# A conv-seq block on one core: LayerNorm transposes by VectorE in 32x32 blocks and through DRAM instead of by TensorE

## The chip, the cores and the metric

The kernel runs on one core of one Trainium2 chip. The metric is device time in microseconds (us), the median of several executions. The core has five engines that run beside each other and meet at semaphores: TensorE (PE in the profile; its weight loads are shown apart as PEld), VectorE (DVE), ScalarE (ACT), GpSimd (POOL) and SyncE (SP), which here only issues DMAs.

## What is computed

The input is `x` of 2 x 256 x 128 x 128 in float32: batch, time T, band FB, channel C. Three sublayers follow each other, each with a LayerNorm in front and a residual sum behind it:

```python
xt = _ln(x, ln_t_w, ln_t_b).transpose(0, 2, 1, 3)
x = x + _mha(xt, t_wi, t_bi, t_wo, t_bo, H_T, cm).transpose(0, 2, 1, 3)   # over time, causal, 4 heads of 32
xf = _ln(x, ln_f_w, ln_f_b)
x = x + _mha(xf, f_wi, f_bi, f_wo, f_bo, H_F, bm)                          # over bands, |i - j| <= 16, 4 heads
xn = _ln(x, ln_n_w, ln_n_b)
h = jax.nn.gelu(xn @ w1.T + b1, approximate=False)                         # 128 -> 512
x = x + (h @ w2.T + b2)                                                    # 512 -> 128
```

## The kernel before

**Groups.** The work is cut into groups of 512 tokens (NT = 4 tiles of 128 tokens by 128 channels). There are 384 of them. First come 128 groups of the attention over time (`OverTime`; two bands with all their 256 times each). They write an intermediate `x1` to DRAM. Then come 128 groups of the attention over bands (`OverBands`; four times with all 128 bands) and 128 of the feed-forward layer (`FeedForward`), in turns of 8 and 8: 16 runs of 8 band groups and then the same 8 groups' feed-forward. This document calls these the time stage, the band iterations and the feed iterations.

**Steps of a group.** `load` brings x (one tile for several groups). `statistics` takes mean and variance on DVE (`stats`, `mv`), `root` takes the power -1/2 on POOL (`rstd`), and `normalize` writes `xh` on DVE, with tokens on the partitions. Matrix products need channels on the partitions. So `transpose` turns the four 128x128 tiles of `xh` on PE into a PSUM bank `xp`, and `take_transposed` copies it to SBUF on ACT as `xnT`. From `xnT` come the products `qp`, `kp`, `vp` in an attention group (copied out as `qT`, `kT`, `v`) and `hp` in a feed group. An attention group goes on with the scores `sp` (PE), their exponentials `pt` or `pf` (ACT), masks (POOL `affine_select`; for bands the last head by a DVE product with `band`), row sums `rp` and weighted values `op` (PE; `weigh`), the inverse of the sums by `ln` and `r` (ACT; `invert`), `t`, `u`, `oT` (DVE; `divide`), the output product `yp` (PE; `output`) and the residual sum (DVE; `finish`). In the time stage POOL also adds two blocks of `pt` for the first half of the scores, and DVE for the second (`last_sum`). POOL forms the residual plus bias (`bias`; `rd` in the time stage). A feed group has `hp`, the Gelu `hT` (ACT), `zp` (PE) and the residual sum `res` (DVE).

**Order.** `BoundedPath.run` writes the order out by hand, as a software pipeline: iteration n works on the scores of group n, on the sums of group n-1, on the output of n-2, on `qp`/`kp`/`vp` of n+1, on the LayerNorm of n+2 and n+3, and loads for n+10. PE, DVE, ACT and POOL keep exactly this program order (`InOrder`), so an instruction that waits holds up everything behind it on its engine. Only the DMAs on SP are placed by the scheduler, and SP too runs its list in order. All PSUM tiles share eight banks that are handed out in turn. So a product that opens a bank waits for the reader of the tile eight openings earlier.

**Numerics.** All is float32. An ordinary product shows as two MATMULs in the trace, a transpose as one.

Another path for large weights (`shifted_path`) is in the program and isn't taken with these inputs.

Of the kernel before, what the change touches and what calls it, by code (L numbers as in the profile page):

```python
# [2 lines left out]

# [6 lines left out]
F32 = mybir.dt.float32  # L10
# [8 lines left out]
P = 128  # L19
H = 4  # L20
# [402 lines left out]


class Group:


# [78 lines left out]
    def take_key(self):  # L506
        pass
# [23 lines left out]
class Attention(Group):  # L531
    which = None

    def bias(self):
        self.dst_tile()
# [4 lines left out]
    def dst_tile(self):  # L540
        pass

# [57 lines left out]
    def finish(self):  # L600
        self.path.vector.tensor_tensor(self.dst(), self.yp, self.dst(), ALU.add)
        if self.store is not None:
            self.store(self.dst())


def rows_of(h):
    return slice(h * D, (h + 1) * D)


class OverTime(Attention):  # L610
# [5 lines left out]
    W = 3 * P  # L616

    def dst_tile(self):
        rd = self.path.work.tile([P, NT, P], F32, name="rd", bufs=5)
        self.dst = lambda: rd  # L620

# [80 lines left out]
class OverBands(Attention):  # L702
# [33 lines left out]

    def take_key(self):
        path = self.path
        self.kT = path.work.tile([P, NT * P], F32, name="kT")
        path.scalar.copy(self.kT, self.kp)  # L740

    def first_half(self):
# [19 lines left out]
class FeedForward(Group):  # L762

    def bias(self):
        path = self.path
        self.res = path.work.tile([P, NT, P], F32, name="res")
        path.gpsimd.tensor_tensor(
            self.res, self.src(), path.k.rows[:, 2:3, :].to_broadcast([P, NT, P]), ALU.add
        )
# [36 lines left out]
    def divide(self):  # L806
        self.path.vector.tensor_tensor(self.res, self.zp, self.res, ALU.add)
        self.store(self.res)

# [16 lines left out]
class BoundedPath:  # L826
    def __init__(self, ctx, tc, k):
# [18 lines left out]
    def bank(self, shape, name):  # L846
        return self.ps.tile(shape, F32, name=name, tag="ps")

    def groups(self, x, out):
        nc, k = self.nc, self.k  # L850
        B, T, FB, C = x.shape
        NC_T = T // P
        S = NT // NC_T
        for b in range(B):
            xv = x[b].rearrange("(o p) f c -> p o f c", p=P)
            x1v = k.x1[b].rearrange("(o p) f c -> p o f c", p=P)
            for f0 in range(0, FB, GA):
                held = {}

                def load(f0=f0, xv=xv, held=held):  # L860
                    held["x"] = self.xpool.tile([P, GA, NC_T, C], F32, name="xt", tag="x")
                    for o in range(NC_T):
                        nc.sync.dma_start(held["x"][:, :, o, :], xv[:, o, f0 : f0 + GA, :])

                for g in range(0, GA, S):

                    def src(g=g, held=held):
                        return held["x"][:, g : g + S].rearrange("p f o c -> p (f o) c")

                    def store(t, f=f0 + g, x1v=x1v):  # L870
                        for o in range(NC_T):
                            nc.sync.dma_start(
                                x1v[:, o, f : f + S, :],
                                t.rearrange("p (f o) c -> p f o c", o=NC_T)[:, :, o, :],
                            )

                    yield OverTime(self, src, None, load if g == 0 else None, store)
        for b in range(B):
            x1v = k.x1[b].rearrange("t f c -> f t c")
            outv = out[b].rearrange("t f c -> f t c")  # L880
            for r0 in range(0, T, RUN):
                run = []
                for t0 in range(r0, r0 + RUN, GB):
                    held = {}

                    def load(t0=t0, x1v=x1v, held=held):
                        held["x"] = self.xpool.tile([P, GB, C], F32, name="xb", tag="x")
                        nc.sync.dma_start(held["x"], x1v[:, t0 : t0 + GB, :])
                        held["x2"] = self.xpool.tile([P, GB, C], F32, name="x2", tag="x2", bufs=2 * RUN // GB)

                    def part(name, g, held=held):
                        return lambda: held[name][:, g : g + NT, :]

                    def store(t, g, outv=outv):
                        nc.sync.dma_start(outv[:, g : g + NT, :], t)

                    run += [(t0 + g, part("x", g), part("x2", g), None if g else load, store) for g in range(0, GB, NT)]
                for i, (_, x_, x2, load, _) in enumerate(run):
                    g = OverBands(self, x_, x2, load)
                    if i == len(run) - 1:  # L900
                        g.by_vector = 2
                    yield g
                for g, _, x2, _, store in run:
                    yield FeedForward(self, x2, None, None, lambda t, g=g, store=store: store(t, g))

    def run(self, x, out):
# [9 lines left out]

        self.scalar.preload_act_table_set(EXP_SET)
        for n in range(-10, len(groups) + 2):
            feeds = [at(n - 2 + i, FeedForward) for i in range(5)]
            bands = [at(n - 2 + i, OverBands) for i in range(5)]  # L920
            do(n + 10, "load")
            do(n + 3, "statistics")
            if bands[2] and feeds[1]:
                self.scalar.preload_act_table_set(EXP_SET)
            do(n, "first_half", "first_function", "first_mask")
            do(n + 2, "normalize")
            do(n + 3, "root")
            if bands[2]:
                do(n, "second_mask")
            if feeds[2] and feeds[3]:  # L930
                do(n + 1, "transpose", "take_transposed")
            do(n - 1, "weigh")
# [4 lines left out]
            do(n - 1, "divide")  # L937
            if feeds[3] and not feeds[2]:
                do(n + 1, "transpose", "take_transposed")
            do(n, "second_half", "second_function")  # L940
            if not bands[2]:
                do(n, "second_mask", "bias")
                if at(n + RUN // NT, OverBands):
                    do(n + RUN // NT, "bias")
                do(n - 2, "output", "finish")
            do(n + 1, "queries_keys", "take_query", "take_key", "values", "take_values")
            do(n, "last_sum")
            if at(n + 2, Attention):
                do(n + 2, "transpose", "take_transposed")

# [68 lines left out]
```

## Time and profile before

| | |
|---|---|
| median of 3 executions | 2968.1 us (2967.6 to 2968.57) |
| the profiled execution | 2968.23 us, of which its span is 2966.3 us |
| busy share of the span | PE 99%, DVE 65%, ACT 68%, POOL 69% |
| granted clock of TensorE | 0.999 of full speed |
| DMA | 140.41 MB, 16.0% of the 16 DMA engines' time on the SP queue |

Rows give the line as L821 for everything that `InOrder` records, so tile names, not lines, tell operations apart (in the changed kernel the same line is L827). A row of the timeline has the start in us from the span's start, the duration, the engine, the operation with its tiles and shapes, the count of merged instructions and, in brackets, the idle time before it and what ended it. A row of the groups has the count, the busy time in all, the mean duration in ns, and the idle time before. PE rows overlap, because matmuls are pipelined: the time that a step costs on PE is the distance from its start to the next start.

### The profile page before, as it was taken

What the parts mean: (1) busy time and instruction counts of PE and PEld (TensorE: products, weight loads), DVE (VectorE), ACT (ScalarE), POOL (GpSimd) and SP (SyncE); (2) the same over time, 40 slices, a digit from 0 to 9 for tenths busy, and PEclk for the clock granted to TensorE, in tenths of its full rate; (3) what the DMA queues carried; (4) which work ended last, traced back from release to release, by engine and by line L of the source; (5) the groups of instructions that cost most, each with busy time, mean ns of one, the idle gap of its engine ahead of it and who ended that gap; (6) DMA issues with size and microseconds to landing.
All of it is one profiled execution on the core that took longest, in us unless ns stands there. A gap on an engine that the chain in (4) does not pass through costs nothing.

```text
span 2966.3 us, 75357 instructions
## 1 busy us (share of the span) xinstructions
PE 2929.6 (99%) x30246; PEld 2082.9 (70%) x30246; DVE 1933.7 (65%) x6206; ACT 2007.6 (68%) x3664; POOL 2057.4 (69%) x2537
## 2 busy tenths in 40 slices
PE   7999999999999999999999999999999999999998
PEld 5666666666666677777777777777777777767776
DVE  6777777777777895646647557466465475564663
ACT  4777777777777776756657657567576576675664
POOL 5888888888888896656657656566576575665662
PEclk9999999999999999999999999999999999999999
DMA  3222222222222221111111111111101011111001
GB/s 84 64 62 62 76 62 62 73 66 62 63 79 62 62 69 37 37 44 30 44 29 37 40 34 41 40 33 41 42 28 48 26 37 40 33 41 44 15 16 30
DMA packets 222855, 140.41 MB, mean 47 GB/s; under 512 B 7968, under 2 KB 205984, under 8 KB 222496
## 3 DMA queue, kind: packets, MB, share of 16 engines
q1 hardware_dynamic: 221248, 134.45, 16.0%
q8 instruction: 240, 3.93, 0.6%
q10 hardware_dynamic: 1248, 1.05, 0.1%
q14 instruction: 119, 0.97, 0.1%
HBM read 68.36 MB, written 67.11 MB: 46 GB/s over the span
## 4 chain that ended last, share of the span: by engine, by line
PE 99%; ACT 0%; DMA 0%; DVE 0%; POOL 0%; issue 0%; SPq 0%; ACTq 0%; POOLq 0%; DVEq 0%
PE zp L821 16%; PE hp L821 15%; PE sp L821 12%; PE op L821 9%; PE yp L821 9%; PE rp L821 9%; PE vp L821 8%; PE qp L821 8%; PE kp L821 7%; PE xp L821 6%; ACT xnT L821 0%; DMA xt<-in_x 0%; DMA f_wiT_sb<-in_f_wiT 0%; POOL pt L821 0%; POOL rstd L821 0%
## 5 line engine op out<-in xcount | busy, mean ns | idle before, releaser
L821 POOL TENSOR_SCALAR_AFFINE_SELECT pf<-pf 128x512 f32<-128x512 f32 x736 | 508.2, 705 | 277.1 <-ACT pf L821 252.0
L821 ACT ACTIVATE hT<-hp,b 128x512 f32<-128x512 f32 x512 | 346.6, 687 | 463.7 <-PE hp L821 460.2
L821 PE MATMUL hp<-xnT,w1f 128*128 128x512 f32 x1024 | 474.4, 596 | 10.8 <-ACT xnT L821 10.8
L821 POOL TENSOR_TENSOR rstd<-rstd,mhalf 128x4 f32<-128x4 f32 x384 | 460.6, 1200 | 32.0
L821 PE MATMUL zp<-w2T_sb,hT 128*128 128x128 f32 x4096 | 480.3, 276 | 0.1
L821 PEld LDWEIGHTS zp<-w2T_sb,hT 128*128 128x128 f32 x4096 | 469.0, 192 | 10.2 <-issue 8.1
L821 ACT ACTIVATE pt<-sp 128x384 f32<-128x384 f32 x1024 | 419.7, 497 | 75.2 <-PE sp L821 42.3
L821 POOL TENSOR_SCALAR_AFFINE_SELECT pt<-pt 128x512 f32<-128x512 f32 x512 | 312.7, 632 | 153.0 <-ACT pt L821 153.0
L821 PE MATMUL sp<-qT,kT 32*128 32x128 f32 (+1 forms) x8192 | 389.6, 316 | 0.0
L821 DVE TENSOR_TENSOR res<-zp,res 128x512 f32<-128x512 f32 x128 | 88.3, 690 | 452.9 <-issue 365.6
L821 POOL TENSOR_SCALAR rstd<-mv 128x4 f32<-128x4 f32 x384 | 94.2, 245 | 397.1 <-DVE mv L821 397.1
L821 PEld LDWEIGHTS sp<-qT,kT 32*128 32x128 f32 x8192 | 311.3, 185 | 72.5 <-issue 40.1
L821 PEld LDWEIGHTS vp<-wf,xnT 128*128 128x128 f32 x2048 | 269.2, 192 | 122.4 <-issue 113.8
L821 DVE TENSOR_TENSOR t<-rp,r 128x512 f32<-128x512 f32 x256 | 175.4, 685 | 215.0 <-ACT r L821 213.4
L821 ACT ACTIVATE pf<-sp 128x512 f32<-128x512 f32 x512 | 264.3, 603 | 57.2 <-POOL rstd L821 32.5
L821 PEld LDWEIGHTS hp<-xnT,w1f 128*128 128x128 f32 x1024 | 180.1, 191 | 171.0 <-issue 151.6
L821 PE MATMUL yp<-wn,oT 128*128 128x128 f32 x2048 | 293.4, 287 | 0.0
L821 PEld LDWEIGHTS yp<-wn,oT 128*128 128x128 f32 x2048 | 250.6, 191 | 49.8 <-issue 18.6
L821 DVE TENSOR_TENSOR pf<-pf,band 128x512 f32<-128x512 f32 x144 | 142.6, 999 | 214.4 <-ACT pf L821 214.4
L821 PE MATMUL vp<-wf,xnT 128*128 128x128 f32 x2048 | 270.0, 275 | 0.0
L821 ACT COPY v<-vp 128x512 f32<-128x512 f32 x256 | 149.8, 585 | 173.9 <-PE vp L821 173.9
L821 PE MATMUL qp<-xnT,wf 128*128 128x512 f32 x512 | 265.0, 600 | 0.7 <-ACT xnT L821 0.7
(94 smaller groups left out, 5053.1 us busy)
## 6 DMA issues: line engine op xcount, KB each, us to landing
xt<-in_x SPq DMA_DIRECT2D x64, 512.0 KB, 5.4
x<-rd SPq DMA_DIRECT2D x256, 128.0 KB, 1.9
out<-res SPq DMA_DIRECT2D x128, 256.0 KB, 2.3
xb<-x SPq DMA_DIRECT2D x32, 0.5 KB, 6.1
w1T_sb<-in_w1T ACTq DMA_DIRECT2D x1, 256.0 KB, 3.8
w2T_sb<-in_w2T ACTq DMA_DIRECT2D x1, 256.0 KB, 4.2
t_wiT_sb<-in_t_wiT ACTq DMA_DIRECT2D x1, 192.0 KB, 2.6
f_wiT_sb<-in_f_wiT ACTq DMA_DIRECT2D x1, 192.0 KB, 3.7
```

Of the source, the lines that this page charges most:

```text
L821: return self.tc.keep_in_program_order(emit(*args, **kwargs))
```

## The change

1. The PE transposes (`xp`) and the ACT copies `xnT<-xp` go, in all 384 groups. In their place `turn` transposes 32x32 blocks of `xh` within each of the four 32-partition rows on DVE, one instruction of 128x512 into a tile `z`. Four DMAs of 64 KB each, one for each 32-partition row, write `z` to a DRAM tile `turned`. `fetch` reads the 256 KB back as `xnT` with one DMA over 128 partitions. `turn` is done three iterations ahead and `fetch` two.
2. A 32x32 transpose can't move data between 32-partition rows. So tokens lie differently on the chip: a group's partition row i holds 32 tokens of each of four stretches, instead of a tile holding 128 neighbours. Loads and stores go in four DMAs over 32 partitions each, for four groups (loads) or two groups (stores) at a time. `xnT` has its columns in the old token order. `t`, `u` and the Gelu's `hT` are written in the new one (`by_rows`), so that the output products give rows in the new layout.
3. In the time stage `kT<-kp` moves from DVE to ACT (in the band iterations it is on ACT already). `output` and `finish` of group n-2 move behind `queries_keys` of n+1.
4. The residual tile is `res`, four groups wide, in both the time stage and the feed iterations. Loads are issued 11 iterations ahead and statistics taken 4 ahead.

```diff
-        self.xh = path.work.tile([P, NT, P], F32, name="xh", bufs=4)
+        self.xh = path.work.tile([P, NT, P], F32, name="xh", bufs=2)
...
-    def transpose(self):
-
-        path = self.path
-        self.xp = path.bank([P, NT * P], "xp")
+    def turn(self):
+
+
+        path = self.path
+        z = path.work.tile([P, H, P], F32, name="z", bufs=2)
+        path.vector.transpose(
+            z.rearrange("p c (t q) -> p c t q", q=D), self.xh.rearrange("p t (c q) -> p c t q", q=D)
+        )
+        self.turned = path.dram.tile([H, D, NT, P], F32, name="turned")
         for i in range(NT):
-            path.tensor.transpose(self.xp[:, i * P : (i + 1) * P], self.xh[:, i, :], path.k.ident)
-
-    def take_transposed(self):
+            path.nc.sync.dma_start(self.turned[:, :, i, :].rearrange("c a x -> a c x"), z[rows_of(i)])
+
+    def fetch(self):
         path = self.path
         self.xnT = path.work.tile([P, NT * P], F32, name="xnT")
-        path.scalar.copy(self.xnT, self.xp)
+        path.nc.sync.dma_start(self.xnT, self.turned.rearrange("c a i x -> (c a) (i x)"))
...
-        path.vector.tensor_copy(self.kT, self.kp)
+        path.scalar.copy(self.kT, self.kp)
...
-        vector.tensor_tensor(t, self.rp, self.r0, ALU.mult)
+        vector.tensor_tensor(by_rows(t), by_tile(self.rp), by_tile(self.r0), ALU.mult)
         u = path.work.tile([P, NT * P], F32, name="u", bufs=2)
-        vector.tensor_tensor(u, self.op, self.r0, ALU.mult)
+        vector.tensor_tensor(by_rows(u), by_tile(self.op), by_tile(self.r0), ALU.mult)
...
-            path.scalar.activation(self.hT[:, j, :], self.hp[j], AF.Gelu, bias=path.k.b1[:, j : j + 1], scale=1.0)
+            path.scalar.activation(
+                by_rows(self.hT[:, j, :]), by_tile(self.hp[j]), AF.Gelu,
+                bias=path.k.b1[:, j : j + 1], scale=1.0,
+            )
...
+        self.dram = ctx.enter_context(tc.tile_pool(name="turns", bufs=3, space=DRAM))
...
+                    for i in range(2 * g, min(2 * g + 2, NT)):
+                        f = f0 + i // NC_T * NT
+                        nc.sync.dma_start(held["x"][rows_of(i)], self.of_times(x[b], i, slice(f, f + NT)))
...
+                    for i in range(NT if g % 2 else 0):
+                        f = f0 + i // NC_T * NT + g
+                        nc.sync.dma_start(
+                            self.of_times(k.x1[b], i, slice(f - 1, f + 1)), held["res"][rows_of(i), :, g - 1 : g + 1]
+                        )
...
-            do(n + 10, "load")
-            do(n + 3, "statistics")
+            do(n + 11, "load")
+            do(n + 4, "statistics")
...
-            do(n + 2, "normalize")
-            do(n + 3, "root")
+            do(n + 2, "fetch")
+            do(n + 3, "normalize", "turn")
+            do(n + 4, "root")
...
-            if feeds[2] and feeds[3]:
-                do(n + 1, "transpose", "take_transposed")
...
-            if feeds[3] and not feeds[2]:
-                do(n + 1, "transpose", "take_transposed")
...
+            do(n + 1, "queries_keys", "take_query", "take_key")
+            if not bands[2]:
                 do(n - 2, "output", "finish")
-            do(n + 1, "queries_keys", "take_query", "take_key", "values", "take_values")
+            do(n + 1, "values", "take_values")
             do(n, "last_sum")
-            if at(n + 2, Attention):
-                do(n + 2, "transpose", "take_transposed")
```

The order on three engines shows what the scheduler made of it. PE, one iteration of the time stage (the second scores, the output of an earlier group, the products of the next group, its first scores), before:

```order
L821 MATMUL sp<-qT,kT 128x128 x4
L821 MATMUL yp<-wn_106,oT 128x128 x4
L821 MATMUL qp<-xnT,wf_103 128x512
L821 MATMUL kp<-xnT,wf_103 128x512
L821 MATMUL vp<-wf_103,xnT 128x128 x4
L821 MATMUL xp<-ident,xh 128x128 x4
L821 MATMUL sp<-qT,kT 128x256 x4
L821 MATMUL sp<-qT,kT 128x128 x4
L821 MATMUL rp<-pt,ones 32x512 x4
```

And of the change:

```order
L827 MATMUL sp<-qT,kT 128x128 x4
L827 MATMUL qp<-xnT,wf_103 128x512
L827 MATMUL kp<-xnT,wf_103 128x512
L827 MATMUL yp<-wn_106,oT 128x128 x4
L827 MATMUL vp<-wf_103,xnT 128x128 x4
L827 MATMUL sp<-qT,kT 128x256 x4
L827 MATMUL sp<-qT,kT 128x128 x4
L827 MATMUL rp<-pt,ones 32x512 x4
```

The four transposes are gone, and `yp` stands between `kp` and `vp`.

DVE in the same stage, from `divide` to the next `divide`, before:

```order
L821 SCALAR_TENSOR_TENSOR oT<-t,u 128x512
L821 TENSOR_TENSOR rd<-yp,rd 128x512
L821 COPY kT<-kp 128x512
L821 TENSOR_TENSOR pt<-pt 128x4x128
L821 BN_STATS stats<-xt 128x6 x4
L821 BN_AGGR mv<-stats 128x2 x4
L821 TENSOR_SCALAR xh<-xt,mv,rstd 128x128 x4
L821 TENSOR_TENSOR t<-rp,r_1795 128x512
```

And of the change (the residual tile is now `res`):

```order
L827 SCALAR_TENSOR_TENSOR oT<-t,u 128x512
L827 TENSOR_TENSOR res<-yp,res 128x4x128
L827 TENSOR_TENSOR pt<-pt 128x4x128
L827 BN_STATS stats<-x 128x6 x4
L827 BN_AGGR mv<-stats 128x2 x4
L827 TENSOR_SCALAR xh<-x,mv,rstd 128x128 x4
L827 STREAM_TRANSPOSE z<-xh 128x512
L827 TENSOR_TENSOR t<-rp,r_1738 128x4x4x32
```

The copy of `kT` has left DVE, and the block transpose stands between `xh` and `t`.

SP's list of DMAs for four groups of the time stage, of the change (before, the same stretch held two loads and eight stores):

```order
L489 DMA turned<-z 32x4x128 x4
L494 DMA xnT<-turned 128x512
L489 DMA turned<-z 32x4x128 x4
L494 DMA xnT<-turned 128x512
L890 DMA x_0_85<-res 32x4x256 x4
L489 DMA turned<-z 32x4x128 x4
L494 DMA xnT<-turned 128x512
L489 DMA turned<-z 32x4x128 x4
L494 DMA xnT<-turned 128x512
L890 DMA x_0_85<-res 32x4x256 x4
L885 DMA x<-in_x 32x4x512 x4
```

Each `fetch` stands right behind the four writes that it must wait for, so SP holds everything behind it until they have landed.

More of the change, by code (lines that the diff above doesn't have):

```diff
@@ L2 @@
 from contextlib import ExitStack
+from functools import partial
 import concourse.bass as bass
@@ L422, in fold, with by_rows, by_tile @@
     return nc.values_load(flag[0:1, 0:1], min_val=0, max_val=1)
+def by_rows(t):
+    return t.rearrange("p (t i q) -> p i t q", i=NT, q=D)
+def by_tile(t):
+    return t.rearrange("p (i t q) -> p i t q", i=NT, q=D)
 class Group:
@@ L534, in bias @@
     def bias(self):
-        self.dst_tile()
         self.path.gpsimd.tensor_tensor(
@@ L538, in bias @@
         )
-    def dst_tile(self):
-        pass
     def queries_keys(self):
@@ L602, in finish @@
         if self.store is not None:
-            self.store(self.dst())
+            self.store()
 def rows_of(h):
@@ L735, in second_mask @@
             path.vector.tensor_tensor(blk, blk, path.band.unsqueeze(1).to_broadcast([P, NT, P]), ALU.mult)
-    def take_key(self):
-        path = self.path
-        self.kT = path.work.tile([P, NT * P], F32, name="kT")
-        path.scalar.copy(self.kT, self.kp)
     def first_half(self):
@@ L765, in bias @@
         path = self.path
-        self.res = path.work.tile([P, NT, P], F32, name="res")
         path.gpsimd.tensor_tensor(
-            self.res, self.src(), path.k.rows[:, 2:3, :].to_broadcast([P, NT, P]), ALU.add
+            self.dst(), self.src(), path.k.rows[:, 2:3, :].to_broadcast([P, NT, P]), ALU.add
         )
@@ L806, in divide @@
     def divide(self):
-        self.path.vector.tensor_tensor(self.res, self.zp, self.res, ALU.add)
-        self.store(self.res)
+        self.path.vector.tensor_tensor(self.dst(), self.zp, self.dst(), ALU.add)
+        self.store()
 class InOrder:
@@ L847, in bank, with of_times, of_bands, quad @@
         return self.ps.tile(shape, F32, name=name, tag="ps")
+    @staticmethod
+    def of_times(ap, i, f):
+        o = ap.shape[0] // P
+        return ap.rearrange("(o t q) f c -> o q t f c", o=o, q=D)[i % o][:, :, f]
+    @staticmethod
+    def of_bands(ap, a, n):
+        return ap[a : a + n].rearrange("t (m q) c -> q (t m) c", q=D)
+    def quad(self, held, name, bufs):
+        held[name] = self.xpool.tile([P, NT, NT, P], F32, name=name, tag=name, bufs=bufs)
     def groups(self, x, out):
@@ L852, in groups, with load @@
         NC_T = T // P
-        S = NT // NC_T
         for b in range(B):
-            xv = x[b].rearrange("(o p) f c -> p o f c", p=P)
-            x1v = k.x1[b].rearrange("(o p) f c -> p o f c", p=P)
             for f0 in range(0, FB, GA):
                 held = {}
[L860 to L877, printed above, removed]
+                def load(g, f0=f0, b=b, held=held):
+                    if g == 0:
+                        self.quad(held, "x", 4)
+                    for i in range(2 * g, min(2 * g + 2, NT)):
+                        f = f0 + i // NC_T * NT
+                        nc.sync.dma_start(held["x"][rows_of(i)], self.of_times(x[b], i, slice(f, f + NT)))
@@ new lines, in store, with part @@
+                def store(g, f0=f0, b=b, held=held):
+                    for i in range(NT if g % 2 else 0):
[3 more added lines that the diff above has]
+                        )
+                def part(name, g, held=held):
+                    if name == "res" and name not in held:
+                        self.quad(held, "res", 2)
+                    return held[name][:, :, g]
@@ L878, in groups @@
+                for g in range(NT):
+                    yield OverTime(self, partial(part, "x", g), partial(part, "res", g), partial(load, g), partial(store, g))
         for b in range(B):
-            x1v = k.x1[b].rearrange("t f c -> f t c")
-            outv = out[b].rearrange("t f c -> f t c")
             for r0 in range(0, T, RUN):
@@ L884, in groups @@
                     held = {}
[L886 to L889, printed above, removed]
-                    def part(name, g, held=held):
-                        return lambda: held[name][:, g : g + NT, :]
-                    def store(t, g, outv=outv):
-                        nc.sync.dma_start(outv[:, g : g + NT, :], t)
@@ L897, in groups, with load @@
-                    run += [(t0 + g, part("x", g), part("x2", g), None if g else load, store) for g in range(0, GB, NT)]
-                for i, (_, x_, x2, load, _) in enumerate(run):
-                    g = OverBands(self, x_, x2, load)
+                    def load(g, t0=t0, b=b, held=held):
+                        if g == 0:
+                            self.quad(held, "x", 4)
+                            self.quad(held, "x2", 2 * RUN // GB)
+                        for i in range(2 * g, min(2 * g + 2, NT)):
+                            nc.sync.dma_start(
+                                held["x"][rows_of(i)].rearrange("q g t c -> q (g t) c"),
+                                self.of_bands(k.x1[b], t0 + NT * i, NT),
+                            )
@@ new lines, in store @@
+                    def store(g, t0=t0, b=b, held=held):
+                        for i in range(NT if g % 2 else 0):
+                            nc.sync.dma_start(
+                                self.of_bands(out[b], t0 + NT * i + g - 1, 2),
+                                held["res"][rows_of(i), g - 1 : g + 1].rearrange("q g t c -> q (g t) c"),
+                            )
+                    def part(name, g, held=held):
+                        if name == "res" and name not in held:
+                            self.quad(held, "res", 2)
+                        return held[name][:, g]
@@ L900, in groups @@
+                    run += [(g, part, load, store) for g in range(NT)]
+                for i, (g, part, load, _) in enumerate(run):
+                    group = OverBands(self, partial(part, "x", g), partial(part, "x2", g), partial(load, g))
                     if i == len(run) - 1:
[L901 to L904, printed above, removed]
+                        group.by_vector = 2
+                    yield group
@@ L906, in run @@
+                for g, part, _, store in run:
+                    yield FeedForward(self, partial(part, "x2", g), partial(part, "res", g), None, partial(store, g))
     def run(self, x, out):
@@ L917, in run @@
         self.scalar.preload_act_table_set(EXP_SET)
-        for n in range(-10, len(groups) + 2):
+        for n in range(-11, len(groups) + 2):
             feeds = [at(n - 2 + i, FeedForward) for i in range(5)]
             bands = [at(n - 2 + i, OverBands) for i in range(5)]
-            do(n + 10, "load")
-            do(n + 3, "statistics")
+            do(n + 11, "load")
+            do(n + 4, "statistics")
             if bands[2] and feeds[1]:
```

3 lines of the change are left out of this document (removed).

## The prediction

> **What bounds the kernel now.** I read the page first: busy shares, and the chain that ended last.
>
> ```profile
> PE 2929.6 (99%) x30246; PEld 2082.9 (70%) x30246; DVE 1933.7 (65%) x6206; ACT 2007.6 (68%) x3664; POOL 2057.4 (69%) x2537
> PE 99%; ACT 0%; DMA 0%; DVE 0%; POOL 0%; issue 0%; SPq 0%; ACTq 0%; POOLq 0%; DVEq 0%
> PE zp L821 16%; PE hp L821 15%; PE sp L821 12%; PE op L821 9%; PE yp L821 9%; PE rp L821 9%; PE vp L821 8%; PE qp L821 8%; PE kp L821 7%; PE xp L821 6%; ACT xnT L821 0%; DMA xt<-in_x 0%; DMA f_wiT_sb<-in_f_wiT 0%; POOL pt L821 0%; POOL rstd
> ```
>
> TensorE is the bound: its busy time is the span, and the chain runs from PE to PE. The transposes `xp` are 6% of that chain, some 178 us. The other engines' 65 to 69% are averages over three stages. So I went to the timeline of each stage for two things: what a transpose really costs on PE, and how much room the others keep once an iteration is shorter.
>
> **What PE loses.** One iteration of the time stage, PE alone:
>
> ```profile
> 399.89 0.94 PE L821 MATMUL sp<-qT,kT 32*128 32x256 f32 x16
> ...
> 403.05 0.94 PE L821 MATMUL sp<-qT,kT 32*128 32x256 f32 x16
> ...
> 406.63 1.05 PE L821 MATMUL vp<-wf,xnT 128*128 128x128 f32 x8
> 407.52 0.60 PE L821 MATMUL xp<-ident,xh 128*128 128x128 f32 x4
> 408.05 0.94 PE L821 MATMUL sp<-qT,kT 32*128 32x256 f32 x16
> 408.91 1.07 PE L821 MATMUL rp<-pt,ones 128*32 128x512 f32 x8
> ```
>
> From the first `sp` to that of the next iteration it is 8.16 us. `xp` takes 0.53 to the next start, but `vp` straight to `sp` isn't free: the last band iteration of each run happens to have no `xp` there.
>
> ```profile
> 2058.80 1.02 PE L821 MATMUL kp<-xnT,wf 128*128 128x512 f32 x2
> 2059.66 1.05 PE L821 MATMUL vp<-wf,xnT 128*128 128x128 f32 x8
> 2060.55 0.60 PE L821 MATMUL xp<-ident,xh 128*128 128x128 f32 x4
> 2061.08 1.17 PE L821 MATMUL sp<-qT,kT 32*128 32x128 f32 x32
> ...
> 2065.91 1.02 PE L821 MATMUL kp<-xnT,wf 128*128 128x512 f32 x2
> 2066.76 1.05 PE L821 MATMUL vp<-wf,xnT 128*128 128x128 f32 x8
> 2067.75 1.17 PE L821 MATMUL sp<-qT,kT 32*128 32x128 f32 x32
> ```
>
> From `kp` to `sp` it is 2.28 us with the transposes and 1.84 without: **0.44 us** a group. A feed iteration agrees (from `xp` to `zp` 0.43):
>
> ```profile
> 1994.76 0.60 PE L821 MATMUL xp<-ident,xh 128*128 128x128 f32 x4
> 1995.19 3.74 PE L821 MATMUL zp<-w2T_sb,hT 128*128 128x128 f32 x32
> ```
>
> 384 groups by 0.44 are **169 us**. The time iteration becomes 7.72 us. A band iteration becomes 6.67, which is 2061.08 to 2067.75 above. `yp`, which only changes places, costs PE the same.
>
> At the head of each feed run PE waits for `xnT` (the list of waits), and ACT is what comes next there, with table loads and these Gelus, which the first `zp` needs (the timeline of ACT):
>
> ```profile
> PE hp L821 <- ACT xnT L821: 10.8, 16, 0.7
> ```
>
> ```profile
> 2081.34 2.42 ACT L821 ACTIVATE hT<-hp,b 128x512 f32<-128x512 f32 x4
> ```
>
> PE arrives at that `zp` earlier by three transposes (1.3 us) and the 0.7 of the wait. ACT gets there earlier only by two `xnT` copies of 0.588 (next rows), 1.2 us. So I count the 0.7 as moved, not gone.
>
> **What is added, and what hides it.**
>
> ```profile
> L821 ACT COPY xnT<-xp 128x512 f32<-128x512 f32 x384 | 225.7, 588 | 11.6 <-PE xp L821 9.2
> L821 ACT COPY kT<-kp 128x512 f32<-128x512 f32 x128 | 74.9, 585 | 19.2 <-PE kp L821 19.2
> L821 DVE COPY kT<-kp 128x512 f32<-128x512 f32 x128 | 88.5, 692 | 61.8 <-PE kp L821 61.7
> L406 DVE TENSOR_SCALAR w1f<-w1T_sb,cols_sb 128x512 f32<-128x512 f32 x1 | 0.5, 465 | 0.0
> ```
>
> ACT: in the time stage 0.585 for `kT` replaces 0.588 for `xnT`, elsewhere 0.588 simply goes. After `kp`, PE has `yp` and `vp` to do before it needs `kT`, and in the row of 2067.75 it went on at once with `vp` alone. Cost nothing.
>
> DVE: no row shows a block transpose. The nearest below is a one-source 128x512 (0.465), the nearest above two passes of the `kT` copy (1.38). I take one pass, 0.69, as it too moves 512 columns from one source. `t`, `u` and `hT` keep their element counts. No row shows their output order; I take no difference, and the upper end of 1.38 stands for it too. In the time stage `kT` leaves DVE, so it does as much as before, and there is a gap in the right place, 1.41 us between `xh` and `t` (the timeline of DVE):
>
> ```profile
> 401.23 1.08 DVE L821 TENSOR_SCALAR xh<-xt,mv,rstd 128x128 f32<-128x128 f32 x4
> 403.71 0.69 DVE L821 TENSOR_TENSOR t<-rp,r 128x512 f32<-128x512 f32 x1 [1.41 <-ACT r L821]
> ...
> 407.44 0.97 DVE L821 TENSOR_TENSOR pt<-pt 128x512 f32<-128x512 f32 x1
> ```
>
> POOL at the same time:
>
> ```profile
> 402.60 1.22 POOL L821 TENSOR_SCALAR_AFFINE_SELECT pt<-pt 128x512 f32<-128x512 f32 x2 [1.22 <-ACT pt L821]
> ...
> 406.64 1.22 POOL L821 TENSOR_SCALAR_AFFINE_SELECT pt<-pt 128x512 f32<-128x512 f32 x2
> ```
>
> The tight chain there is POOL's. From its first select (402.60) through the second pair (406.64) to DVE's sum `pt` (ends 408.41), and then `rp` at 408.91: 0.50 us spare. The iteration loses 0.44, so **0.06** is left. `yp` now starts two products later, so `finish` ends only just ahead of that sum; and as the sum ends later against `sp`, `xh` runs into POOL's first select. Either could cost 0 to 0.2 us an iteration. I take 0.06, **8 us** in 128, and keep 0 and 26 for the range.
>
> In the bands DVE has no `kT` to lose:
>
> ```profile
> 2043.09 1.04 DVE L821 TENSOR_TENSOR pf<-pf,band 128x512 f32<-128x512 f32 x1 [1.31 <-ACT pf L821]
> ...
> 2050.20 1.04 DVE L821 TENSOR_TENSOR pf<-pf,band 128x512 f32<-128x512 f32 x1 [1.49 <-ACT pf L821]
> ```
>
> Of 7.11 us it idles 1.49, so it works 5.62. With 0.69 that is 6.31 of 6.67. I allow 0.06 for collisions, **8 us**; the ends are 0 and, at 1.38, 7.00 - 6.67 = 0.33, 42 us. Feed iterations have neither chain, and DVE only sums there.
>
> The Trainium skill, "VectorE: DVE Perf Modes", section "The three transpose paths", gives 311 ns for a DVE transpose of 128x128 in bf16. An estimate from that page in proportion to columns is 1.24 us, by which the bands would lose 0.19 us an iteration, 24 us in place of 8. No row of this trace shows it.
>
> SP and the DMAs:
>
> ```profile
> L872 SPq DMA_DIRECT2D x<-rd x256: 359/415/1580, 55.5 to 1091.7; - x128
> DMA to landing us min/median/max: 1.8/1.9/5.4
> ```
>
> A group now has four writes, one fetch, two stores and one load, 8 issues of 0.415 or 3.3 us, and SP stands still while the writes land, 1.9: 5.2 us of 7.72. So SP keeps up. From `z` to `xnT` it is 4 x 0.415 + 1.9 + 0.415 + 1.9 = 5.9 us, and `turn` runs about two iterations (15 us) ahead of `qp`. Queued behind SP's wait are only the next writes, stores and loads, each with an iteration to spare.
>
> Start and end:
>
> ```profile
> 25.97 1.15 PE L821 MATMUL xp<-ident,xh 128*128 128x128 f32 x4 [10.61 <-DVE xh L821]
> ```
>
> The first group has no cover: 0.69 and 5.9 in place of PE's `xp` and ACT's copy (about 1.9), and 16 loads of 256 KB stand ahead of the first write on SP. **+6 us**, between 3 and 12. The last store is four issues, **+1**.
>
> The sum, against the profiled execution (2968.23, span 2966.3, 1.9 around it; the median of the runs shown is 2968.1): 2966.3 - 169 + 8 + 8 + 6 + 1 + 1.9 = **2822 us**.
>
> **The rivals.**
>
> *DVE becomes the bound of the bands* (2845 to 2890). Place: the band iterations; it decides from a transpose of 1.05 us on (6.67 - 5.62). At 1.38: 2822 - 8 + 42 = 2856; with 0.2 us more in each of the 256 attention iterations from DVE and POOL in each other's way, 2890. For it: 5% of room. Against it: the gap between `xh` and `pf` is where the transpose goes.
>
> *SP becomes the bound, and the kernel is slower.* One mechanism: SP is held by each fetch until the four writes have landed. It loses against before once landing takes over 8.16 - 3.3 = 4.8 us in the time stage. At the row's worst, 5.4, a time iteration takes 8.7 and any other (104 issues in 16 groups, 6.5 each) 5.4 + 6.5 x 0.415 = 8.1, so 128 x 8.7 + 256 x 8.1 + 30 for the start = 3220. For it: loads of 1 MB queue ahead on the same rings every four groups. Against it: the median is 1.9.
> The Trainium skill, "DMA: Bandwidth & Descriptors", section "Rules for kernel authors", speaks against this change: under 64 KB one pays mostly overhead, and transfers to disjoint partition ranges serialize. Four landings of 1.9 in turn would make 7.6, and by the same sum some 3500. The trace doesn't bear it out for stores: they go out in pairs, and yet the median landing is 1.9, hardly above the least, 1.8, where every second one would show twice that.
>
> *The change does what it says and gains nothing*: `xnT` comes late and PE waits 0.44 for it instead of turning it. 2966. It needs 15 us between `z` and `xnT` instead of 5.9.
>
> *More than forecast* (under 2800): the feed heads give back their 10.8 us and nothing collides: 2822 - 16 - 11 = 2795.
>
> **How the numbers follow.** Forecast (2800 to 2845) 0.60; DVE bound 0.20; under 2800 0.05; between 2890 and 2962 0.03; no gain 0.02; SP bound 0.10. The range takes the first two and most of the third, 2794 to 2890. A measurement of this kernel can tell 0.2%, about 6 us, from no change: faster 0.88, same 0.02, slower 0.10.
>
> **What would show it.** The time iteration from `sp` to `sp` at 7.7 to 7.8 us, the band iteration at 6.7, `zp` straight behind `hp` in the feeds; the row of `z` near 690 ns; PE still 98% or more and no row of PE waiting for a DMA beyond the first groups. Wrong would be: `z` above 1.05 us, a wait of `rp` for DVE of more than 0.2 us an iteration, or fetches landing later than their `qp`.

## The result and the profile after

| | before | after |
|---|---|---|
| time, median (us) | 2967.85 | 2886.28 |
| profiled execution, span (us) | 2966.3 | 2884.5 |
| first `qp` on PE | 27.86 | 40.94 |
| time stage, first `qp` to first `sp` of the bands | 1049.6 | 999.7 |
| bands and feeds, from there to the last `zp` | 1878.1 | 1830.9 |
| last `zp` to the end | 10.8 | 13.0 |

The ratio is 0.9725, with a 95% interval of 0.9706 to 0.9744. The prediction was 2822, so 82 us were gained where 146 were forecast. The parts add up: +13.1 at the start, -49.9 in the time stage, -47.2 in bands and feeds, +2.2 at the end, together -81.8. One of the four executions of the changed kernel took 2947.33 us, 61 more than the others, at the same granted clock; it is left out of the ratio and has no trace.

First the page of the changed kernel: busy times, and the chain that ended last.

```profile
PE 2830.8 (98%) x28710; PEld 1992.5 (69%) x28710; DVE 2214.7 (77%) x6462; ACT 1864.6 (65%) x3408; POOL 2022.5 (70%) x2537
PE 72%; DVE 21%; POOL 4%; DMA 1%; issue 1%; ACT 0%; SPq 0%; ACTq 0%; DVEq 0%; POOLq 0%
```

PE's 98% hides the loss: the time for which a product stalls counts as busy (the `sp` rows of the bands below take 1.93 us, and 1.17 before). The chain doesn't: it was PE alone, and now 21% of it runs through DVE. Of DVE's and SP's new groups the page says (columns: busy, mean ns of one, idle before; of the DMAs KB each and us to landing):

```profile
L827 DVE STREAM_TRANSPOSE z<-xh 128x512 f32<-128x512 f32 x384 | 273.2, 711 | 18.6 <-DMA turned<-z 5.4
...
turned<-z SPq DMA_DIRECT2D x1536, 64.0 KB, 1.8
xnT<-turned SPq DMA_DIRECT2D x384, 256.0 KB, 2.7
```

The block transpose takes 0.711 us, near the 0.69 that was taken. The writes land in 1.8 us and the fetch in 2.7 (medians). The list of waits has one row of PE waiting for a fetch, the first:

```profile
PE qp L827 <- DMA xnT<-turned: 25.5, 1, 25.5
```

So the way through DRAM is hidden. Nor does a write wait for the landing of the one before it. From the first write of a group to the fetch, which waits for all four, SP's rows have 3.21 us, where four landings in turn would take 7.2:

```profile
1976.93 1.77 SPq L489 DMA_DIRECT2D turned<-z  x4
1980.14 0.34 SPq L494 DMA_DIRECT2D xnT<-turned  x1
```

Now the iterations, PE alone: time stage, feeds, bands.

```profile
403.00 0.94 PE L827 MATMUL sp<-qT,kT 32*128 32x256 f32 x16
...
410.76 0.94 PE L827 MATMUL sp<-qT,kT 32*128 32x256 f32 x16
```

```profile
1918.63 3.60 PE L827 MATMUL hp<-xnT,w1f 128*128 128x512 f32 x8
1925.63 3.60 PE L827 MATMUL hp<-xnT,w1f 128*128 128x512 f32 x8
...
1985.81 1.93 PE L827 MATMUL sp<-qT,kT 32*128 32x128 f32 x32
1993.24 1.93 PE L827 MATMUL sp<-qT,kT 32*128 32x128 f32 x32
```

The time iteration is 7.76 us (8.16 before), the feed iteration 7.00 (7.44: 1983.88 to 1991.32 before), both as forecast. The band iteration is **7.43 us, in place of the 6.67 forecast, and longer than the 7.11 of before**, without the transposes. It settles there from the fifth iteration of a run on; the third still takes 6.67 (1971.34 to 1978.01) and the fourth 7.80. From the first `sp` of a band run to its first `hp` it is 54.74 us (1958.08 to 2012.82), 54.48 before (1900.94 to 1955.42): the bands gained nothing at all. `sp` itself takes 1.93 in place of 1.17. PE's weight loads show who holds it:

```profile
1985.81 0.47 PEld L827 LDWEIGHTS sp<-qT,kT 32*128 32x128 f32 x6
1986.59 0.96 PEld L827 LDWEIGHTS sp<-qT,kT 32*128 32x128 f32 x26 [0.30 <-DVE t L827]
```

It wants a PSUM bank that DVE has not yet read with `t`. Why is DVE late? Its timeline over one iteration, and POOL's selects of the same one:

```profile
1986.46 0.68 DVE L827 TENSOR_TENSOR u<-op,r 128x512 f32<-128x512 f32 x1
1987.17 0.69 DVE L827 SCALAR_TENSOR_TENSOR oT<-t,u 128x512 f32<-128x512 f32 x1
1987.78 0.86 DVE L827 BATCH_NORM_STATS2 stats<-x 128x6 f32<-128x128 f32 x4
1988.56 0.36 DVE L827 BATCH_NORM_AGGREGATE mv<-stats 128x2 f32<-128x6 f32 x4
1988.84 2.17 DVE L827 TENSOR_SCALAR xh<-x,mv,rstd 128x128 f32<-128x128 f32 x4
1991.05 0.71 DVE L827 STREAM_TRANSPOSE z<-xh 128x512 f32<-128x512 f32 x1
1991.68 1.08 DVE L827 TENSOR_TENSOR pf<-pf,band 128x512 f32<-128x512 f32 x1
```

```profile
1988.29 3.93 POOL L827 TENSOR_SCALAR_AFFINE_SELECT pf<-pf 128x512 f32<-128x512 f32 x6 [1.74 <-ACT pf L827]
```

There is no gap in DVE's row. The window over this iteration (columns: PE, PEld, DVE, ACT, POOL, clock, DMA, GB/s):

```profile
1985.81:1993.24 7.43, 7.32 (x93) 5.13 (x93) 7.36 (x19) 5.04 (x9) 5.40 (x9) 1.00 0.37 104
```

DVE is busy 7.36 of 7.43 us, where 6.31 was the forecast. The difference is `xh`: 2.17 us, beside POOL's selects, and 1.08 in the kernel before, where it ended 0.06 us ahead of them:

```profile
2047.63 1.08 DVE L821 TENSOR_SCALAR xh<-xb,mv,rstd 128x128 f32<-128x128 f32 x4
```

```profile
2048.77 4.25 POOL L821 TENSOR_SCALAR_AFFINE_SELECT pf<-pf 128x512 f32<-128x512 f32 x6 [1.22 <-ACT pf L821]
```

### The profile page after: what moved, and what is told of

It reads as the page before. It is cut to its first block, busy times and chain, and to the rows that moved or that the text cites. A ratio compares the mean times of both kernels' runs of the same rounds, so it can differ in the third digit from the quotient of the medians.

```text
span 2884.5 us, 76036 instructions
## 1 busy us (share of the span) xinstructions
PE 2830.8 (98%) x28710; PEld 1992.5 (69%) x28710; DVE 2214.7 (77%) x6462; ACT 1864.6 (65%) x3408; POOL 2022.5 (70%) x2537
## 3 DMA queue, kind: packets, MB, share of 16 engines
q10 hardware_dynamic: 1248, 1.05, 0.1%
## 4 chain that ended last, share of the span: by engine, by line
PE 72%; DVE 21%; POOL 4%; DMA 1%; issue 1%; ACT 0%; SPq 0%; ACTq 0%; DVEq 0%; POOLq 0%
PE zp L827 16%; PE hp L827 15%; PE sp L827 9%; PE op L827 7%; DVE xh L827 7%; PE rp L827 5%; PE qp L827 5%; PE yp L827 5%; PE vp L827 5%; PE kp L827 4%; DVE pf L827 3%; POOL pf L827 2%; DVE z L827 2%; DVE stats L827 2%; DVE t L827 2%; DVE x L827 2%
## 5 line engine op out<-in xcount | busy, mean ns | idle before, releaser
L827 POOL TENSOR_SCALAR_AFFINE_SELECT pf<-pf 128x512 f32<-128x512 f32 x736 | 466.8, 649 | 307.4 <-ACT pf L827 282.2
L827 DVE TENSOR_SCALAR xh<-x,mv,rstd 128x128 f32<-128x128 f32 x1536 | 545.3, 416 | 25.5 <-POOL rstd L827 25.5
L827 PE MATMUL sp<-qT,kT 32*128 32x128 f32 (+1 forms) x8192 | 447.7, 319 | 11.0 <-ACT kT L827 0.8
L827 POOL TENSOR_TENSOR rstd<-rstd,mhalf 128x4 f32<-128x4 f32 x384 | 432.5, 1126 | 32.0
L827 PEld LDWEIGHTS sp<-qT,kT 32*128 32x128 f32 x8192 | 350.5, 185 | 91.4 <-DVE t L827 25.0
L827 POOL TENSOR_SCALAR rstd<-mv 128x4 f32<-128x4 f32 x384 | 129.1, 336 | 352.0 <-DVE mv L827 352.0
L827 DVE BATCH_NORM_STATS2 stats<-x 128x6 f32<-128x128 f32 x1536 | 330.6, 276 | 7.4 <-DMA x<-in_x 7.4
L827 PE MATMUL qp<-xnT,wf 128*128 128x512 f32 x512 | 277.7, 624 | 25.5 <-DMA xnT<-turned 25.5
L827 DVE STREAM_TRANSPOSE z<-xh 128x512 f32<-128x512 f32 x384 | 273.2, 711 | 18.6 <-DMA turned<-z 5.4
L827 PE MATMUL yp<-wn,oT 128*128 128x128 f32 x2048 | 280.5, 280 | 0.0
```

Of the source, the lines that this page charges most:

```text
L827: return self.tc.keep_in_program_order(emit(*args, **kwargs))
```

## The experiments

Three theories on the bands: **A**, `xh` has come to lie on POOL's selects, the two hold each other up, and that makes DVE the bound; **B**, the block transpose is simply too much work for DVE; **C**, the rotation of PSUM banks alone makes `sp` wait. A time given without an interval is one execution; the kernel before took 2969.4 beside the first four and 2967.9 beside the next four.

### DVE's order swapped

```diff
-            do(n + 4, "statistics")
...
             do(n + 3, "normalize", "turn")
+            do(n + 4, "statistics")
```

> The same instructions; only the statistics of group n+4 go behind xh and z of group n+3 in DVE's order, so that xh comes ahead of POOL's six selects and the statistics run beside them. Theory A (the block transpose stands in front, so that DVE's xh falls on POOL's selects, the two hold each other up, xh 2.17 us in place of 1.08, and DVE becomes the bound): xh back to about 1.1, the band iteration from 7.43 to about 6.7, about 2810 us in all. Theory B (DVE simply has too much work in a band iteration): nothing changes, about 2886. Theory C (sp waits for banks that DVE reads late, whatever xh does): xh gets shorter, the band iteration stays above 7.2, about 2880.

2852.3 us, 34 less than the change where A expected 76. PE's `sp` rows of one band run, and the two `xh` rows of DVE that belong to them:

```profile
1955.15 1.17 PE L827 MATMUL sp<-qT,kT 32*128 32x128 f32 x32
1961.82 0.49 PE L827 MATMUL sp<-qT,kT 32*128 32x128 f32 x4
1962.97 1.75 PE L827 MATMUL sp<-qT,kT 32*128 32x128 f32 x28 [0.66 <-DVE x L827]
1970.22 1.23 PE L827 MATMUL sp<-qT,kT 32*128 32x128 f32 x32
1976.95 1.17 PE L827 MATMUL sp<-qT,kT 32*128 32x128 f32 x32
```

```profile
1957.32 2.64 DVE L827 TENSOR_SCALAR xh<-x,mv,rstd 128x128 f32<-128x128 f32 x4 [1.25 <-POOL rstd L827]
...
1971.48 1.43 DVE L827 TENSOR_SCALAR xh<-x,mv,rstd 128x128 f32<-128x128 f32 x4
```

The same instructions in another order run at 6.67 to 6.73 us once settled, so B falls. But the fourth iteration takes 8.40, after an `xh` that waited for `rstd` and then lay wholly on the selects.

### Two sets of PSUM banks

```diff
-        self.ps = ctx.enter_context(tc.tile_pool(name="ps", bufs=8, space=PSUM))
+        self.ps = ctx.enter_context(tc.tile_pool(name="ps", bufs=4, space=PSUM))
...
-        return self.ps.tile(shape, F32, name=name, tag="ps")
+        return self.ps.tile(shape, F32, name=name, tag="sp" if name in ("sp", "hp") else "ps")
```

> The change with two sets of four PSUM banks, one for sp and hp, one for the rest, in place of one rotation of eight: sp no longer waits for a bank that DVE's t or u reads. Theory C: sp takes 1.1 us again, the band iteration is 6.7 and the whole about 2810. Theory A: xh keeps its collision with the selects (about 2.1 us) and DVE stays busy all the time, so that only the place of PE's wait moves (from sp to rp), 7.3 to 7.4 us, about 2880; unless the shifted phase frees xh, which its row would show. Theory B: as A, but with xh at 1.1.

2935.8 us, longer than any theory had it. In the bands `sp` is 1.17 again and `xh` lies ahead of the selects:

```profile
1922.44 1.08 DVE L827 TENSOR_SCALAR xh<-x,mv,rstd 128x128 f32<-128x128 f32 x4
1923.56 0.71 DVE L827 STREAM_TRANSPOSE z<-xh 128x512 f32<-128x512 f32 x1
1924.88 1.04 DVE L827 TENSOR_TENSOR pf<-pf,band 128x512 f32<-128x512 f32 x1 [0.61 <-ACT pf L827]
```

yet the iteration is 6.98 us (1921.54 to 1928.52): the other products now share four banks, and the weight load of `kp` waits 0.87 us for DVE's sum `x`, which reads the bank of `yp`. And the time stage went to 8.25 us an iteration (402.36 to 410.61), by a wait that the change doesn't have there:

```profile
PE rp L827 <- DVE pt L827: 61.1, 128, 1.1
```

The time stage takes 1060.6 us in place of 999.7, which is more than the whole kernel is longer than the change. One execution doesn't show that the edit brings this about: the change, without any edit, has one that is 61 us longer. The kernel changes two things at once, and decides nothing between A and C by itself.

### Without the block transposes

```diff
-        z = path.work.tile([P, H, P], F32, name="z", bufs=2)
-        path.vector.transpose(...)
+        z = self.xh
```

`xh` gets three buffers here in place of two.

> Leaves the block transposes out (z is xh, so that what TensorE multiplies is not transposed); the DRAM way and all else stay. Theories A and B: DVE gets 0.71 us an iteration back, the band iteration is 6.7, about 2805 to 2810 in all. Theory C: the band iteration stays near 7.4, about 2880.

2851.0 us; A and B expected 2805 to 2810. Here is the surprise: with DVE relieved of 0.71 us, `xh` still lies on the selects.

```profile
1977.47 2.21 DVE L824 TENSOR_SCALAR xh<-x,mv,rstd 128x128 f32<-128x128 f32 x4
```

So the meeting doesn't need the transpose. The kernel before has it too, once in each run of bands (in 15 of the 16 in the third iteration), and is out of it in the next:

```profile
1916.81 2.21 DVE L821 TENSOR_SCALAR xh<-xb,mv,rstd 128x128 f32<-128x128 f32 x4 [0.19 <-POOL rstd L821]
1923.12 1.08 DVE L821 TENSOR_SCALAR xh<-xb,mv,rstd 128x128 f32<-128x128 f32 x4
```

In the change it begins in the third iteration as well, and stays:

```profile
1973.52 2.64 DVE L827 TENSOR_SCALAR xh<-x,mv,rstd 128x128 f32<-128x128 f32 x4 [0.19 <-POOL rstd L827]
```

What differs is the length of the loop. In the meeting DVE has, by an estimate from its rows, 5.62 + 1.09 = 6.7 us of work in an iteration without the block transpose, and 0.71 more with it. The 7.11 us of before leave it room to catch up, so that `xh` gets ahead of the selects again. With `xp` gone the 6.67 us leave none: DVE is busy 6.78 of 6.81 us here (1863.68 to 1870.49) and 7.36 of 7.43 in the change. Without the transposes the loss is small (iterations of 6.80 to 6.90 us, a band run of 51.64), with them it is large (7.43, 54.74). The total of this kernel says less than its band rows, since its time stage is 14 us longer than that of the change (1013.9 for 999.7), and why is open.

### Without POOL's selects

The six selects of a band iteration are left out, so three heads go without their band mask.

```diff
-            for s in (1, -1):
-                path.gpsimd.affine_select(...)
+            path.gpsimd.memset(blk[:, 0:1, 0:1], 1.0)
```

> Leaves out POOL's six selects of each band iteration (the band mask of three heads; a set of one column stands in their place), and leaves DVE all of its work. Theory A: xh has nobody beside it, 1.1 us, the band iteration is 6.7, about 2810. Theories B and C: xh at 1.1 too, but DVE's work or the banks keep the band iteration near 7.4, about 2880.

2821.4 us. DVE has all its work, transposes included:

```profile
1951.95 0.87 DVE L823 BATCH_NORM_STATS2 stats<-x 128x6 f32<-128x128 f32 x4
1952.74 0.36 DVE L823 BATCH_NORM_AGGREGATE mv<-stats 128x2 f32<-128x6 f32 x4
1953.02 1.09 DVE L823 TENSOR_SCALAR xh<-x,mv,rstd 128x128 f32<-128x128 f32 x4
1954.14 0.71 DVE L823 STREAM_TRANSPOSE z<-xh 128x512 f32<-128x512 f32 x1
1955.26 0.69 DVE L823 TENSOR_TENSOR pf<-pf,band 128x512 f32<-128x512 f32 x1 [0.41 <-ACT pf L823]
```

```profile
1951.93 1.17 PE L823 MATMUL sp<-qT,kT 32*128 32x128 f32 x32
...
1958.60 1.17 PE L823 MATMUL sp<-qT,kT 32*128 32x128 f32 x32
```

6.67 us with the one rotation of banks: B and C both fall, and A stands. (The edit takes POOL's work away too; the kernel with `rstd` ahead of the selects, below, keeps that work and has 6.67 as well.) A band run takes 50.58 us, 4.16 less than in the change; in 16 runs that is 67 us, and the whole differs by 65. The multiplication `pf` falls from 1.08 to 0.69 too, so it had also been paying for the selects. These rows also say where the selects would lie in a loop of 6.67 us. They start 1.43 us ahead of `pf` (2048.77 and 2050.20 before), so by this estimate at 1953.83, and `xh` ends at 1954.11. In DVE's old order the shorter loop puts `xh` onto them by 0.28 us in every iteration.

### Fewer loads ahead of the first group

SP's loads and its writes of `turned` are kept in the order of the program; then

```diff
-            do(n + 11, "load")
+            for m in [n + 7] if n < 1 else range(8, 13) if n == 1 else [n + 11]:
+                do(m, "load")
```

> The change with SP's loads and its writes of turned blocks kept in the order of the program, and the loads 7 groups ahead instead of 11 until the first group starts: 6 loads of 256 KB ahead of the first write instead of 16. If the late start (first qp at 40.94 us, 25.87 for the first transposes of TensorE before) comes from the 4 MB that stand ahead of the first writes on the DMA engines, the first qp comes at 33 to 35 and the whole is 6 to 8 us shorter, about 2879. If the start is the length of the new way itself (writes, landing, fetch), it stays at 40 and the time at 2886. If SP's fixed order holds it up later, rows of TensorE waiting for xnT appear and the time is longer.

2880.4 us, and the first `qp`:

```profile
35.36 2.05 PE L827 MATMUL qp<-xnT,wf 128*128 128x512 f32 x2 [20.20 <-DMA xnT<-turned]
```

That is 5.6 us earlier, and the whole is 5.8 shorter, a little less than expected. In the change 16 loads of 256 KB stand ahead of the first write, SP's first eight writes take 8.33 us to issue, and the first fetch comes behind all eight:

```profile
16.91 11.53 SPq L885 DMA_DIRECT2D x<-in_x  x16
29.44 8.33 SPq L489 DMA_DIRECT2D turned<-z  x8
```

Here the first fetch follows the first four writes, so the edit changes two things, and how much of the 5.6 us belongs to the loads isn't shown. 7.5 us of the later start (35.36 against 27.86) remain, with six loads still ahead of the first write; how much of them is the new way itself is open.

### `rstd` ahead of the selects

The swap, with the statistics one group earlier in all stages, and in the bands `rstd` ahead of the selects:

```diff
-            do(n + 4, "statistics")
+            do(n + 5, "statistics")
...
+            if bands[2]:
+                do(n + 4, "root")
             do(n, "first_half", "first_function", "first_mask")
```

> The swap, and besides in the bands POOL's rstd of the next group ahead of its six selects instead of behind them, for which the statistics are made one group earlier. The swap left one long iteration a run (8.40 us in place of 6.67, the fourth), after an xh that had waited 1.25 us for rstd and then fell on the selects (2.64 us). If that wait is what pushes xh onto the selects, the long iteration goes, about 1.7 us in each of 16 runs, 2852 becomes about 2825. If the meeting of xh and the selects comes about without it, the run stays near 2852.

2824.5 us. The long iteration is gone. In the settled iterations DVE's `xh` and POOL's selects now miss each other:

```profile
1955.82 1.11 DVE L827 TENSOR_SCALAR xh<-x,mv,rstd 128x128 f32<-128x128 f32 x4
```

```profile
1957.59 4.25 POOL L827 TENSOR_SCALAR_AFFINE_SELECT pf<-pf 128x512 f32<-128x512 f32 x6 [0.62 <-ACT pf L827]
```

```profile
1955.68:1962.35 6.67, 6.67 (x94) 4.68 (x93) 6.30 (x19) 5.04 (x9) 5.76 (x9) 1.00 0.62 177
```

This is the kernel of the forecast: DVE works 6.30 us of 6.67. In the time stage the same order puts `xh` beside POOL's work, 2.07 us (at 403.39) in place of the 1.08 of the change, and the iteration is 7.72 all the same: DVE works 6.91 of it, so there the meeting fits in.

### The copy of `kT` left on DVE

```diff
-        path.scalar.copy(self.kT, self.kp)
+        if isinstance(self, OverTime):
+            path.vector.tensor_copy(self.kT, self.kp)
+        else:
+            path.scalar.copy(self.kT, self.kp)
```

> The change with the kT copy of the time stage left on DVE, as before. If ACT's taking it is what makes room for the block transpose there (DVE works 6.33 of 7.76 us an iteration, 7.0 with the copy, and its sum pt is just in time for rp), rp waits for pt, and the iteration becomes 7.9 to 8.4 us, 20 to 80 us in all. If DVE's free 1.09 us between oT and res takes it in, the time iteration stays at 7.76 and the whole at 2886.

2891.1 us, 5 more than the change. The time iteration is 7.73 us (387.95 to 395.68), so DVE's gap between `oT` and `res` does take the copy in. The 5 us lie at the end of the time stage (1004.3 us for 999.7): its last seven iterations take 8.62 to 9.20 us where the change has 7.96 to 8.13.

### `rstd` alone

As two experiments above, without the swap.

> The early rstd of the bands without the swap: the statistics (one group earlier) stay ahead of xh and z in DVE's order. If xh has to come ahead of the statistics to find POOL free or to catch up, xh stays near 2.2 us, the band iteration near 7.4 and the time near 2886. If the late rstd was the whole of it, the bands are at 6.67 and the time is near 2825, as with the swap.

2953.5 us. The bands stay at 7.43 (1949.87 to 1957.30), so there the early `rstd` needs the swap. What makes this kernel longer than the change is the time stage, 1061.7 us for 999.7. It falls into the rhythm of the two bank sets, 8.30 us (400.50 to 408.80):

```profile
PE rp L827 <- DVE pt L827: 62.3, 128, 2.2
```

There DVE's sum `pt`, a product of two tiles that lies beside POOL's work, takes 1.47 us (0.69 in the kernel with both edits), and `rp` waits half a microsecond for it, every iteration. As with the two bank sets, one execution doesn't show that the edit brings this rhythm about. Without the 62 us the kernel would be near 2891.

### All that helped, together

> The swap, the early rstd and the fewer early loads together. If the three add up: bands at 6.67 and the first qp at 33 to 35, about 2818; if the early rstd does nothing, about 2845.

2820.6 us: the parts add up to within 3 us.

> The kernel of the swap, the early rstd and the fewer early loads once more, timed: 2820.6 us in the single look, against 2968 of the kernel before 0.950.

2817.9 us, the ratio to before 0.9493 (95% interval 0.948 to 0.9506), against 0.9725 for the change as it was made. The page of this kernel has DVE busier than that of the change, and PE less:

```profile
PE 2769.0 (98%) x28710; PEld 1932.3 (69%) x28710; DVE 2262.1 (80%) x6462; ACT 1865.7 (66%) x3408; POOL 2045.4 (73%) x2537
```

## Why the prediction was partly right

- **0.44 us a group for TensorE's transposes: right.** Feeds lost 0.44 an iteration, the time stage 0.40. Where the selects are left out, all three stages run as forecast, and the time is 2821.4 against the 2822 predicted. That it comes so close is luck: the start took 7 us more than its term, and of the 8 us for collisions in the bands nothing was used.
- **The block transpose, 0.69: right**, 0.711. From the 311 ns of the Trainium skill ("VectorE: DVE Perf Modes", "The three transpose paths") the prediction had an estimate of 1.24 by proportion; the measurement decides against that use of the figure.
- **SP and the way through DRAM hidden: right.** No wait after the first group. The four writes of a group land in 1.8 us each, and 3.21 us after the first of them the fetch goes out. So none waits for the landing of another, and the rival in which SP is the bound falls. Its second price was also mis-added: with 7.6 us for the landings the same sum is 128 x 10.9 + 256 x 10.3 + 30, some 4060 and not 3500.
- **Time stage, +0.06 an iteration: right**, 7.76 where 7.72 plus 0.06 was forecast. That `kT` leaves DVE is not what makes room for the transpose: the gap holds both in the settled iterations, as the run with the copy on DVE shows, and the move is worth 5 us.
- **Bands, "I allow 0.06 for collisions, 8 us": this step failed.** It cost 67 us. DVE's sum of 6.31 was right (6.30 in the kernel with both edits), but a sum of busy time takes each duration as fixed. The prediction counted DVE's idle 1.49 as room, without laying POOL's row beside it, as it did in the time stage. `xh` ended 0.06 us ahead of the selects, and in a loop shorter by 0.44 it falls on them. Then `xh` takes 2.17, DVE has no slack left, `t` and `u` free the banks late, `sp` waits for them, and the selects, which follow `sp`, wait too. So the meeting moves along with the delay, as the rows read, and each settled iteration has it again. The kernel before had the meeting too, once in each run, and had the room to get out of it.
- On why the two hold each other up, the Trainium skill, "SBUF — State Buffer", section "Who interferes with whom", says: VectorE and GpSimd share one pair of ports, as an exclusive lock, which DVE takes in its two-port modes (`tensor_scalar` is named) or, against a GpSimd instruction that reads SBUF, when it reads two inputs from SBUF. The rows agree: `xh` 2.17 and 1.09, `pf` 1.08 and 0.69, with and without the selects. Which mode `xh` ran in no run here shows.
- **The rival "DVE becomes the bound of the bands"** is what came, at 2886, near the end of its range, but not by its condition: the transpose stayed below 1.05 us. Its second price, 0.2 us in each of 256 attention iterations from DVE and POOL in each other's way, was the mechanism in the wrong place: 0.76 in each settled band iteration, next to nothing in the time stage. So it is in good part luck that 2886 lies inside the range. Its upper end, 2890, doesn't even follow from the rival's own terms, which give 2856 + 256 x 0.2 = 2907.
- **Start, +6: too little**, +13.1. The range of 3 to 12 just missed it. The 16 loads were seen, and the start was priced too low: with ten of them fewer, and the first fetch behind four writes in place of eight, 5.6 us came back.
- **End, +1**: +2.2.

## What to carry to other kernels

A sum of busy times shows that an engine has room, not that its work falls into that room: before counting on a gap, lay the row of the engine that lengthens its instructions (here POOL's) beside the gap, and see by how little they miss each other. Count the work of an iteration in which they meet, too: if it is more than the new loop takes, the engine doesn't get out of the meeting again. When a loop gets shorter, everything that hangs on its head moves against everything that hangs on its tail; a meeting that this brings about can settle in as a steady rhythm, and here the cure was order (a few lines of the schedule), not less work. A share of 98% for TensorE says nothing of stalls within its products; the chain and one iteration do.

## What was not expected of the hardware

- In the meeting of `xh` and the selects it is mostly DVE that pays: `xh` goes from 1.08 to 2.17 us, while six selects take 3.93 us in the change, less than the 4.25 of the kernel before where only `pf` met them. In the one meeting of each run before they take 4.42 with `xh` at 2.21. How long they take with nothing beside them no run shows.
- The time stage has two steady rhythms with nearly the same instructions, 7.7 to 7.8 us and 8.25 to 8.30. The slower one was seen in the kernel with two bank sets and in the one with `rstd` alone (and the statistics one group earlier), with one execution each, so what decides between the two is open. That DVE and POOL meeting at `pt` makes the slower one is read from the rows and not shown otherwise.
